# A graph network's edge sweep: edge products from TensorE taken by VectorE directly, or laid down in SBUF 40 steps ahead

## The chip, the cores and the metric

One of the eight cores of a Trainium2 chip. The metric is the device time of one execution in microseconds; lower is better. The times before are 3401.76, 3403.89 and 3417.29 us (median 3403.89). One further execution was taken by the hardware profiler.

## What is computed

6250 nodes with 256 features, 100,000 edges sorted by destination, 64 features an edge. Three rounds of messages, cut from the reference:

```python
# round 0
e = relu((x[dst] - x[src]) @ theta_w.T + theta_b + x[src] @ phi_w.T + phi_b)
out = segment_max(e, dst);  out = where(isfinite(out), out, 0)
x = layernorm(x + out)
# rounds 1 and 2
hv = x @ W_in + b_in
for W, b in ((W_u0, b_u0), (W_u1, b_u1)):
    m = relu(concatenate([hv[src], edge_attr], -1) @ W + b)
    hv = where(deg > 0, segment_max(m, dst) + hv, hv)
x = layernorm(x + relu(hv @ W_ro + b_ro))
```

Products with x[src] or hv[src] are the same for all edges of one source, so the kernel makes them once a node, as a table in DRAM with a row a node, and each edge gathers its row. Terms that depend on dst alone, and the ReLU, come after the maximum.

## The kernel before

It is written in Bass with the Tile layer, which adds the semaphore waits; under `manual_schedule` each engine runs its instructions in the order in which the program lists them. There is a prologue (the first table, a test that the edges are sorted, a branch) and then `in_order`, which this document is about; the other branch, `any_order`, doesn't run on these inputs.

**Edges.** The sorted edges are laid out in 17 blocks of 128 lanes by 56 steps (the last blocks shorter), 782 steps in all (`FS`). A lane holds consecutive edges, so a running maximum along the steps, reset by `lim` where the destination changes, leaves each segment's maximum at the segment's last edge. `sweep(r)` goes over the 782 steps once a round:

- POOL (GpSimd) issues one indirect DMA a step (`sources`, L719), which gathers 128 rows of 256 floats from `table[r]` into one slot of a `run` tile of 8 steps (`K` = 8). Gathers are listed 16 steps ahead (`AHEAD`). There are four `run` tiles, and one is used again when its write to S has landed.
- In rounds 1 and 2 the edge features' product is added. `features` (L725) loads the features of 8 steps on ACT's DMA queue, up to four tiles; `pair` (L730) makes the product of two steps with one fp32 matmul of 512 columns, into one of two PSUM buffers (tag `he`), one pair ahead; VectorE (DVE) adds it onto two steps of `run` (L923).
- DVE takes the running maximum, one instruction a step (L926).
- SyncE (SP) writes each finished group of 8 steps, 1 MB, to S in DRAM (L932).
- At a block's end `over_lanes` carries the maxima across lanes: transposes on TensorE (PE), a scan on DVE (L746), transposes back, a copy to `cs` on ACT (L758).

**Nodes.** They are treated in 49 tiles of 128. `node(t, g, b)` puts its parts into slots of the steps: `rows` (L771) gathers, on POOL, each node's row of S, at the step where its last block is written; `picks` and `carried` (L783, L790) make the carried maxima `v` with matmuls into PSUM, 3 and 2 steps before slot b; from slot b on, DVE takes the maximum of the two and ACT the ReLU, the result is added, transposed, multiplied by the next weights, and written to the next round's table on ACT's DMA queue. Round 0 also normalises, keeps the new x in `x_sb`, and makes both `hv` and the first update's table; round 2 adds `x_sb` (L853), normalises and writes the output. Tiles follow each other by `gap` = 4, 4 and 6 steps, by 3 after the last step. Whatever is left after the 782 steps is listed in slot order. A round's table must be whole before the next round's first gather.

In round 0 one more thing runs: `count`, every third step for 98 times, builds two one-hot tiles on DVE (`ol` L647, `oh` L650) and sums them on PE (L653); from the counts come `has` and `end_i`, and nodes can begin only then, at step 300.

**Memory.** x (49 tiles, 48 KB a partition) and hv (`h_sb`, the same) stay in SBUF for the whole run.

Of the kernel before, what the change touches and what calls it, by code (L numbers as in the profile page):

```python
# [17 lines left out]
P = 128  # L18
# [5 lines left out]
K = 8  # L24
# [18 lines left out]
KEPT = 7  # L43
# [11 lines left out]
SPAN = [span(t) for t in range(NT)]  # L55

# [377 lines left out]
def gnn_kernel(  # L434
# [6 lines left out]
    table = [dram.tile([ROWS, D], F32, name=f"table{r}") for r in range(3)]  # L441


    jmp = const.tile([P, P], I32)
# [7 lines left out]
    col_i = const.tile([P, P], I32)  # L452
# [97 lines left out]
def in_order(ctx: ExitStack, tc: tile.TileContext, g):  # L550
# [9 lines left out]
    heT, xTn, xn, out = (g[n] for n in ("heT", "xTn", "xn", "out"))  # L560
    ctx.enter_context(tc.manual_schedule())
# [4 lines left out]
    x_sb = one.tile([P, NT, D], F32, name="x_sb")  # L566
# [9 lines left out]
    def weight(w, name):  # L576
        t = one.tile([P, 2, D], F32, name=name)
        nc.scalar.dma_start(t, w.rearrange("(k p) f -> p k f", p=P))
        return t
# [7 lines left out]
    tb, pb = line(g["th_b"], "tb"), line(g["ph_b"], "pb")  # L587
    wcat = one.tile([P, 2, 2 * D], F32, name="wcat")
    nc.scalar.dma_start(wcat[:, :, :D], g["w_in"].rearrange("(k p) f -> p k f", p=P))
    winT = weight(g["w_inT"], "winT")  # L590
    wu0 = weight(g["w_u0"][:D, :], "wu0")
# [7 lines left out]
    whe = []  # L599
    for r, w in enumerate((g["w_u0"], g["w_u1"])):  # L600
        t = one.tile([P, 2, D], F32, name=f"whe{r}")
        nc.vector.memset(t, 0.0)
        for s in range(2):
            nc.scalar.dma_start(t[s * DE:(s + 1) * DE, s, :], w[D:, :])
        whe.append(t)
# [37 lines left out]
    def count(c):  # L643
        k = min(K, FS - c * K)
        cut = slice(c * K, c * K + k)
        ol = work.tile([P, K, P], BF16, name="ol", bufs=1)
        nc.vector.tensor_tensor(ol[:, :k, :], col.unsqueeze(1).to_broadcast([P, k, P]),  # L647
                                lo[:, cut].unsqueeze(2).to_broadcast([P, k, P]), OP.is_equal)
        oh = work.tile([P, K, NT], BF16, name="oh", bufs=1)
        nc.vector.tensor_tensor(oh[:, :k, :], col[:, :NT].unsqueeze(1).to_broadcast([P, k, NT]),  # L650
                                hi[:, cut].unsqueeze(2).to_broadcast([P, k, NT]), OP.is_equal)
        for j in range(k):
            nc.tensor.matmul(hist[:, :NT], ol[:, j, :], oh[:, j, :], start=(c == 0 and j == 0),  # L653
                             stop=(c == NG - 1 and j == k - 1))
# [50 lines left out]
    def sweep(r):  # L705
# [10 lines left out]
        def sources(s):  # L716
            if s % K == 0:
                runs[s // K] = work.tile([P, K, D], F32, name="run", bufs=4)
            nc.gpsimd.indirect_dma_start(  # L719
                out=runs[s // K][:, s % K, :], out_offset=None, in_=table[r],  # L720
                in_offset=bass.IndirectOffsetOnAxis(ap=s_s[:, s:s + 1], axis=0))

        def features(c):
            hT[c] = work.tile([P, K // 2, P], F32, name="hT", bufs=4)
            nc.scalar.dma_start(hT[c].rearrange("p q e -> p (q e)"), heT[c])  # L725

        def pair(i):
            c, q = divmod(i, K // 2)
            hp[i] = psum.tile([P, 512], F32, tag="he", name="hp")
            nc.tensor.matmul(hp[i], hT[c][:, q, :], whe[r - 1].rearrange("p s f -> p (s f)"), start=True, stop=True)  # L730
            if q == K // 2 - 1:
                del hT[c]

        def over_lanes(b, last):

            lp = psum.tile([P, 512], F32, tag="tp", name="lp")
            nc.tensor.transpose(lp[:, 2 * P:3 * P], link[:, b:b + 1].to_broadcast([P, P]), ident)
            lim2 = work.tile([P, P], F32, name="lim2")
            nc.scalar.copy(lim2, lp[:, 2 * P:3 * P])  # L739
            for k in range(2):  # L740
                nc.tensor.transpose(lp[:, k * P:(k + 1) * P], last[:, k * P:(k + 1) * P], ident)  # L741
            to, of = cT[b % 2], cT[(b + 1) % 2]

            def scan():
                for k in range(2):
                    nc.vector.tensor_tensor_scan(to[:, k, 1:], lim2, lp[:, k * P:(k + 1) * P],  # L746
                                                 of[:, k, P:] if b else 0.0, OP.min, OP.max)
                if b:
                    nc.scalar.copy(to[:, :, 0:1], of[:, :, P:])
                else:  # L750
                    nc.vector.memset(to[:, :, 0:1], 0.0)

            def back():
                cp = psum.tile([P, 512], F32, tag="tp", name="cp")
                for k in range(2):
                    nc.tensor.transpose(cp[:, k * P:(k + 1) * P], to[:, k, :P], ident)
                carried_in.append(b)
                nc.scalar.copy(cs[:, b % KEPT, :D], cp[:, :D])  # L758

            at(FIRST[b] + BLOCKS[b], scan)  # L760
            at(FIRST[b] + BLOCKS[b] + 1, back)

        def node(t, g, b):
# [22 lines left out]
            def carried():  # L786
                assert max(carried_in) - SPAN[t][0] < KEPT
                o["v"] = psum.tile([P, 512], F32, tag="v", name="v")
                for blk, p in o["pick"]:
                    nc.tensor.matmul(o["v"][:, :N1], p, cs[:, blk % KEPT, :N1], start=(blk == SPAN[t][0]),  # L790
                                     stop=(blk == SPAN[t][1]))

            def x_in():
                o["xT"] = work.tile([P, 2, P], F32, name="xT", bufs=3)
                nc.sync.dma_start(o["xT"], xTn[:, :, t * P:(t + 1) * P])
# [12 lines left out]
            def first_b():  # L808
                nc.vector.tensor_add(o["m"], o["m"], h_sb[:, t, :])
                nc.scalar.activation(o["m"], o["m"], AF.Relu, scale=has[:, t:t + 1])  # L810

            def first_c():
                nc.vector.tensor_add(o["m"], o["m"], x_sb[:, t, :])
# [4 lines left out]
            def first_e():  # L818
                norm(x_sb[:, t, :], o["m"], *o["mv"])
                o["aT"] = turned(x_sb[:, t, :])  # L820

            def first_f():
                o["g"] = times(o["aT"], wcat[:, :, D:], b2, D)

            def first_g():
                o["ps"] = times(o["aT"], wcat[:, :, :D], None, D)

            def first_h():
                new = work.tile([P, D], F32, name="new", bufs=3)
                nc.scalar.copy(new, o["g"][:, :D])  # L830
                nc.scalar.dma_start(table[1][t * P:(t + 1) * P, :], new)

            def first_i():
                nc.scalar.copy(h_sb[:, t, :], o["ps"][:, :D])

            def next_a():
                nc.vector.tensor_max(o["m"], o["m"], o["v"][:, :D])  # L837
                nc.scalar.activation(o["m"], o["m"], AF.Relu, scale=has[:, t:t + 1])
# [8 lines left out]
            def next_d():  # L847
                new = work.tile([P, D], F32, name="new", bufs=3)
# [3 lines left out]
            def last_d():  # L852
                nc.vector.scalar_tensor_tensor(o["m"], o["ps"][:, :D], 0.0, x_sb[:, t, :], OP.max, OP.add)  # L853

            def last_e():
                o["mv"] = stats(o["m"], "m")

            def last_f():
                o["y"] = work.tile([P, D], F32, name="new", bufs=3)
                norm(o["y"], o["m"], *o["mv"])  # L860
# [4 lines left out]
            at(g, rows)  # L865
            if r == 0:
# [3 lines left out]
            at(b - 3, picks)  # L870
            at(b - 2, carried)
            if r == 0:
                for i, f in ((0, first_a), (1, first_b), (3, first_c), (4, first_d), (6, first_e), (7, first_f),
                             (8, first_g), (9, first_h), (10, first_i)):
                    at(b + i, f)
            else:
                for i, f in ((0, next_a), (2, next_b), (3, next_c)):
                    at(b + i, f)
                for i, f in ((5, next_d),) if r == 1 else ((5, last_d), (6, last_e), (8, last_f), (9, last_g)):
# [3 lines left out]
        if r == 0:  # L883
# [4 lines left out]
            for i in range(NT // PART):  # L888
                at(14 + 8 * i, lambda i=i: nc.sync.dma_start(x_sb[:, i * PART:(i + 1) * PART, :],
                                                             xn[:, i * PART:(i + 1) * PART, :]))  # L890
# [5 lines left out]
        gap = (4, 4, 6)[r]  # L896
        b = 0
        for t in range(NT):
            e = max(FIRST[SPAN[t][1]] + BLOCKS[SPAN[t][1]], begin)
            b = max(b + (gap if b < FS else 3), e + 4, min(e + AHEAD + 4, FS + 4))  # L900
            node(t, max(e, b - AHEAD - 4), b)

        runs, hT, hp = {}, {}, {}
        prev = None
        blk = 0
        for s in range(-AHEAD, FS):
# [5 lines left out]
            if r > 0:  # L912
                if s == 0:
                    for i in range(4):
                        features(i)
                    pair(0)
                elif j == 0 and c + 3 < NG:
                    features(c + 3)
                if s % 2 == 0:
                    if s + 2 < FS:  # L920
                        pair(s // 2 + 1)
                    two = runs[c][:, j:j + 2, :].rearrange("p s f -> p (s f)")
                    nc.vector.tensor_add(two, two, hp.pop(s // 2))  # L923
# [18 lines left out]
    for r in range(3):  # L942
        sweep(r)
# [48 lines left out]
```

## Time and profile before

| | us |
|---|---|
| median of the runs shown | 3403.9 |
| profiled execution, own time | 4092.0 |
| its span | 4090.2 |
| PE busy (matmul) | 2032.6 (50%) |
| PE weight loads | 915.2 (22%) |
| DVE busy | 2083.0 (51%) |
| ACT busy | 280.7 (7%) |
| POOL busy | 2459.6 (60%) |
| mean granted TensorE clock | 0.667 |
| DMA | 735.87 MB, mean 180 GB/s |

The profile is one execution, and it took 688 us more than the median of the runs that weren't profiled: what it shows has to be weighed against that. Busy times are sums over all of the span. A matmul's end is modelled, not seen; an fp32 matmul appears as two records. "Issue" names idle time that ended without a release that the profile shows; "remote" names a release whose source it doesn't know. [...]

### The profile page before, as it was taken

Reading aid. Unit: us, or ns where it says so; the run is one execution under the profiler, and the core shown is the slowest. Engines: PE = TensorE matmul, PEld = TensorE weight load, DVE = VectorE, ACT = ScalarE, POOL = GpSimd, SP = SyncE. Lnnn points to the kernel's source line nnn. Section 1 sums busy time; section 2 is a strip of 40 time slices with the busy share of each in tenths; the row PEclk is TensorE's granted clock in tenths of the full one; section 3 lists DMA queues with packets and bytes.
Section 4 is the critical chain, followed back from the end, with each engine's and each line's share of the span. In section 5 each row is a group of like instructions: output and inputs, shape, how many; then the busy total and the mean of one; then the engine's idle time right before and its main releaser. Section 6 shows DMA issues by size and latency. Waiting matters only on the chain.

```text
span 4090.2 us, 22048 instructions
## 1 busy us (share of the span) xinstructions
PE 2032.6 (50%) x4957; PEld 915.2 (22%) x4957; DVE 2083.0 (51%) x4526; ACT 280.7 (7%) x770; POOL 2459.6 (60%) x2499
## 2 busy tenths in 40 slices
PE   5433444232334745455464555664455545555557
PEld 4222222111112311111121222221121212122223
DVE  2766733433334555454554454545555555555555
ACT  1000010000101100000000000110000000000001
POOL 3777755666664466566666655546666666655542
PEclk7555565555555867676777777786766777777766
DMA  6755544454554456565555555545655555555542
GB/s 223 250 195 181 195 157 169 166 181 161 170 168 147 147 189 211 172 205 179 195 192 184 181 181 183 172 164 191 204 191 193 191 180 192 182 174 171 175 146 86
DMA packets 237763, 735.87 MB, mean 180 GB/s; under 512 B 51880, under 2 KB 91799, under 8 KB 200375
## 3 DMA queue, kind: packets, MB, share of 16 engines
q0 software_dynamic: 119664, 326.92, 26.7%
q1 hardware_dynamic: 66096, 334.71, 21.5%
q10 hardware_dynamic: 51862, 72.75, 5.4%
q8 instruction: 42, 0.69, 0.1%
q14 instruction: 99, 0.80, 0.1%
HBM read 401.01 MB, written 333.16 MB: 179 GB/s over the span
## 4 chain that ended last, share of the span: by engine, by line
another core or an unknown queue 31%; DVE 18%; PE 16%; issue 15%; POOL 9%; DMA 8%; ACT 1%; ACTq 0%; DVEq 0%; POOLq 0%; SPq 0%
POOL run L719 9%; DVE run L926 8%; DVE run L923 7%; DMA run<-table,s_s 5%; PE hp L730 5%; PE prod L700 4%; PE prod L702 2%; PE v L790 2%; DMA S<-run 1%; PE ps L533 1%; PE tp L692 1%; ACT aT L694 1%; DVE pick L783 1%; DMA hT<-in_heT 0%
## 5 line engine op out<-in xcount | busy, mean ns | idle before, releaser
L719 POOL DMA_INDIRECT run<-table,s_s x2346 | 2316.6, 987 | 1294.2 <-issue 696.2
L730 PE MATMUL hp<-whe,hT 128*128 128x512 f32 x1564 | 1054.5, 779 | 589.7 <-DVE run L923 378.2
L926 DVE SCALAR_TENSOR_TENSOR run<-run,lim 128x256 f32<-128x256 f32 x2295 | 1110.6, 484 | 205.7 <-DMA run<-table,s_s 120.5
L923 DVE TENSOR_TENSOR run<-run,hp 128x512 f32<-128x512 f32 x782 | 533.7, 682 | 809.0 <-remote 459.7
L730 PEld LDWEIGHTS hp<-whe,hT 128*128 128x128 f32 x1564 | 308.0, 233 | 1190.7 <-DVE run L923 699.6
L771 POOL DMA_INDIRECT m<-S,end_i x147 | 142.4, 969 | 291.6 <-DMA S<-run 191.4
L700 PE MATMUL prod<-wcat,aT 128*128 128x256 f32 x392 | 160.4, 550 | 261.9 <-ACT aT L694 167.6
L790 PE MATMUL v<-cs,pick 128*128 128x256 f32 (+1 forms) x468 | 192.6, 540 | 123.9 <-DVE pick L783 70.9
L692 PE MATMUL tp<-ident,h_sb 128*128 128x128 f32 x196 | 52.7, 361 | 358.9 <-DVE h_sb L841 223.6
L653 PE MATMUL hist<-oh,ol 128*128 128x49 bf16 x782 | 48.8, 217 | 249.2 <-DVE oh L650 182.2
L700 PEld LDWEIGHTS prod<-wcat,aT 128*128 128x128 f32 x392 | 95.5, 268 | 314.2 <-ACT aT L694 177.6
L790 PEld LDWEIGHTS v<-cs,pick 128*128 128x128 f32 x468 | 116.2, 272 | 199.6 <-issue 83.5
L746 DVE TENSOR_TENSOR_SCAN cT<-lim,cT,lp 128x128 f32<-128x128 f32 x96 | 40.8, 468 | 218.5 <-PE lp L741 144.5
L853 DVE SCALAR_TENSOR_TENSOR m<-prod,x_sb 128x256 f32<-128x256 f32 x49 | 20.8, 424 | 248.9 <-remote 169.9
L700 PE MATMUL prod<-wro,aT 128*128 128x256 f32 x196 | 90.4, 609 | 96.8 <-issue 76.1
L647 DVE TENSOR_TENSOR ol<-col,lo 128x1024 bf16<-128x1024 bf16 x98 | 119.3, 1217 | 26.3 <-remote 25.7
L692 PEld LDWEIGHTS tp<-ident,h_sb 128*128 128x128 f32 x196 | 25.1, 173 | 451.4 <-issue 318.5
L741 PE MATMUL lp<-ident,run 128*128 128x128 f32 x102 | 28.7, 375 | 183.0 <-ACT lim L739 101.5
L700 PE MATMUL prod<-wu,aT 128*128 128x256 f32 x196 | 75.6, 524 | 68.4 <-ACT aT L694 36.7
L837 DVE TENSOR_TENSOR m<-m,v 128x256 f32<-128x256 f32 x98 | 40.5, 414 | 134.9 <-remote 78.1
L653 PEld LDWEIGHTS <-ol 128*128 128x128 bf16 x782 | 42.8, 117 | 276.2 <-DVE ol L647 164.5
L700 PE MATMUL prod<-th,xT 128*128 128x256 f32 x196 | 95.5, 640 | 8.8 <-issue 8.8
(116 smaller groups left out, 1326.0 us busy)
## 6 DMA issues: line engine op xcount, KB each, us to landing
S<-run SPq DMA_DIRECT2D x291, 1024.0 KB
hT<-in_heT ACTq DMA_DIRECT2D x196, 256.0 KB
run<-table,s_s POOLq DMA_INDIRECT x2346
table<-new ACTq DMA_DIRECT2D x98, 128.0 KB
xg<-in_xTn SPq DMA_DIRECT2D x7, 896.0 KB
table<-g SPq DMA_DIRECT2D x7, 896.0 KB
xT<-in_xTn SPq DMA_DIRECT2D x49, 128.0 KB
x_sb<-in_xn SPq DMA_DIRECT2D x7, 896.0 KB
```

The costliest lines, as they stand in the source:

```text
L533: nc.tensor.matmul(ps[:, q * D:(q + 1) * D], xg[:, k, (i + q) * P:(i + q + 1) * P], wd[:, k, :], start=(k == 0), stop=(k == 1))
L647: nc.vector.tensor_tensor(ol[:, :k, :], col.unsqueeze(1).to_broadcast([P, k, P]), lo[:, cut].unsqueeze(2).to_broadcast([P, k, P]), OP.is_e ...
L653: nc.tensor.matmul(hist[:, :NT], ol[:, j, :], oh[:, j, :], start=(c == 0 and j == 0), stop=(c == NG - 1 and j == k - 1))
L692: nc.tensor.transpose(tp[:, k * P:(k + 1) * P], a[:, k * P:(k + 1) * P], ident)
L700: nc.tensor.matmul(ps[:, :n], aT[:, k, :], w[:, k, :], start=(k == 0), stop=(k == 1 and b is None))
L702: nc.tensor.matmul(ps[:, :n], every[0:1, :], b, start=False, stop=True)
L719: nc.gpsimd.indirect_dma_start(out=runs[s // K][:, s % K, :], out_offset=None, in_=table[r], in_offset=bass.IndirectOffsetOnAxis(ap=s_s[:, ...
L730: nc.tensor.matmul(hp[i], hT[c][:, q, :], whe[r - 1].rearrange("p s f -> p (s f)"), start=True, stop=True)
L771: i = nc.gpsimd.indirect_dma_start(out=o["m"], out_offset=None, in_=S_r[:P * (FIRST[SPAN[t][1]] + BLOCKS[SPAN[t][1]]), :], in_offset=bass. ...
L790: nc.tensor.matmul(o["v"][:, :N1], p, cs[:, blk % KEPT, :N1], start=(blk == SPAN[t][0]), stop=(blk == SPAN[t][1]))
L923: nc.vector.tensor_add(two, two, hp.pop(s // 2))
L926: nc.vector.scalar_tensor_tensor(cur, prev, lim[:, s:s + 1], cur, OP.min, OP.max)
```

## The change

**Edge products.** `features` and `pair` become `products(c)`, called five groups (`EARLY` = 5, 40 steps) ahead: it loads the features of group c on SP's queue (three tiles), makes the four pairs of products on PE one after the other, and copies each from PSUM with ACT to a tile `made`, of which there are six. DVE adds four steps of `made` onto `run` with one instruction of 1024 elements, instead of two steps from PSUM with one of 512.

**Nodes.** `carried` copies `v` from PSUM to an SBUF tile (six of them) on ACT. `picks` and `carried` stand 8 and 7 steps before slot b (`calm` = 6), and the scan over lanes and its way back 5 and 6 steps after the block's end instead of 0 and 1. The ReLU with `has` moves from ACT to DVE. `hv` and the table's rows of round 0 come from one product of 512 columns. In round 2 the last ReLU is made by ACT, and the sum with x by DVE six steps later. `gap` is 6 in all rounds.

**Memory.** `x_sb` is gone: x is loaded tile by tile on SP's queue (three tiles), and round 0's result is written to a DRAM tensor `x1` on ACT's queue, and read again in round 2. Weights that are used only at the start lie in a `run` tile; the edge weights `whe` are one tile, loaded before each of the last two rounds.

The diff, cut to its core:

```diff
-KEPT = 7
+RING = 4
+EARLY = 5
+KEPT = 9
...
+def calm(s):
+    return 6
...
-        def features(c):
-            hT[c] = work.tile([P, K // 2, P], F32, name="hT", bufs=4)
-            nc.scalar.dma_start(hT[c].rearrange("p q e -> p (q e)"), heT[c])
-
-        def pair(i):
-            c, q = divmod(i, K // 2)
-            hp[i] = psum.tile([P, 512], F32, tag="he", name="hp")
-            nc.tensor.matmul(hp[i], hT[c][:, q, :], whe[r - 1].rearrange("p s f -> p (s f)"), start=True, stop=True)
-            if q == K // 2 - 1:
-                del hT[c]
+        def products(c):
+
+            hT = work.tile([P, K // 2, P], F32, tag="pt", name="hT", bufs=3)
+            nc.sync.dma_start(hT.rearrange("p q e -> p (q e)"), heT[c])
+            made[c] = work.tile([P, K, D], F32, tag="made", name="made", bufs=EARLY + 1)
+            for q in range(min(K, FS - c * K) // 2):
+                hp = psum.tile([P, 512], F32, tag="he", name="hp")
+                nc.tensor.matmul(hp, hT[:, q, :], whe.rearrange("p s f -> p (s f)"), start=True, stop=True)
+                nc.scalar.copy(made[c][:, 2 * q:2 * q + 2, :].rearrange("p s f -> p (s f)"), hp)
...
-            at(FIRST[b] + BLOCKS[b], scan)
-            at(FIRST[b] + BLOCKS[b] + 1, back)
+            e = FIRST[b] + BLOCKS[b]
+            at(e + calm(e) - 1, scan)
+            at(e + calm(e), back)
...
+                o["v"] = work.tile([P, D + 2], F32, name="vs", bufs=6)
+                nc.scalar.copy(o["v"][:, :N1], v[:, :N1])
+
+            def x_row():
+                o["x"] = work.tile([P, D], F32, name="x", bufs=3)
+                nc.sync.dma_start(o["x"], xn[:, t, :] if r == 0 else x1[t * P:(t + 1) * P, :])
...
-                nc.scalar.activation(o["m"], o["m"], AF.Relu, scale=has[:, t:t + 1])
+                nc.vector.tensor_scalar(o["m"], o["m"], 0.0, has[:, t:t + 1], OP.max, OP.mult)
...
-                norm(x_sb[:, t, :], o["m"], *o["mv"])
-                o["aT"] = turned(x_sb[:, t, :])
+                norm(o["x"], o["m"], *o["mv"])
+                o["aT"] = turned(o["x"])
+                nc.scalar.dma_start(x1[t * P:(t + 1) * P, :], o["x"])
...
             def last_d():
-                nc.vector.scalar_tensor_tensor(o["m"], o["ps"][:, :D], 0.0, x_sb[:, t, :], OP.max, OP.add)
+                o["y"] = work.tile([P, D], F32, name="new", bufs=6)
+                nc.scalar.activation(o["y"], o["ps"][:, :D], AF.Relu)
+
+            def last_dd():
+                nc.vector.tensor_add(o["y"], o["y"], o["x"])
...
-            at(b - 3, picks)
-            at(b - 2, carried)
+            at(b - late - 2, picks)
+            at(b - late - 1, carried)
...
-        gap = (4, 4, 6)[r]
+        gap = 6
...
-                if s % 2 == 0:
-                    if s + 2 < FS:
-                        pair(s // 2 + 1)
-                    two = runs[c][:, j:j + 2, :].rearrange("p s f -> p (s f)")
-                    nc.vector.tensor_add(two, two, hp.pop(s // 2))
+                if j == 0 and c + EARLY < NG:
+                    products(c + EARLY)
+                w = min(4, FS - s)
+                if s % 4 == 0:
+                    four = runs[c][:, j:j + w, :].rearrange("p s f -> p (s f)")
+                    nc.vector.tensor_add(four, four, made[c][:, j:j + w, :].rearrange("p s f -> p (s f)"))
```

## The prediction

> **What bounds the kernel now.** I read, in this order: the profile page (groups and busy times), busy time by stretch for POOL alone, the waits, and the order of time in four short windows. On the page (line, engine, operation; count; busy us, mean ns; idle us before it and what ended it) four groups carry the sweeps:
>
> ```profile
> L719 POOL DMA_INDIRECT run<-table,s_s x2346 | 2316.6, 987 | 1294.2 <-issue 696.2
> L730 PE MATMUL hp<-whe,hT 128*128 128x512 f32 x1564 | 1054.5, 779 | 589.7 <-DVE run L923 378.2
> L926 DVE SCALAR_TENSOR_TENSOR run<-run,lim 128x256 f32<-128x256 f32 x2295 | 1110.6, 484 | 205.7 <-DMA run<-table,s_s 120.5
> L923 DVE TENSOR_TENSOR run<-run,hp 128x512 f32<-128x512 f32 x782 | 533.7, 682 | 809.0 <-remote 459.7
> ```
>
> Each of the 2,346 gathers costs POOL 0.987 us and a fixed gap of 0.30 us that nothing ends ("issue": 2168 of them): 1.29 us a step. DVE needs 0.48 us a step for the running maximum and, in the last two sweeps, 0.34 us for half an edge add: 0.83 us. POOL is the slower of the two by a third. The next view gives POOL's busy time (instructions in brackets), clock, DMA share and GB/s, cut at each sweep's first and last gather:
>
> ```profile
> 0.00:59.85 59.85, 0.61 (x6) 0.98 0.70 253
> 59.85:1338.00 1278.15, 844.02 (x825) 0.53 0.53 179
> 1338.00:1389.96 51.96, 5.67 (x7) 0.90 0.24 82
> 1389.96:2663.54 1273.58, 800.95 (x825) 0.72 0.57 188
> 2663.54:2710.43 46.89, 5.67 (x6) 0.92 0.27 95
> 2710.43:4006.40 1295.97, 796.11 (x824) 0.71 0.55 184
> 4006.40:4090.20 83.80, 6.61 (x7) 0.64 0.18 64
> ```
>
> So the span is a sum on POOL: 59.9 before the first gather; 2441.1 busy in the sweeps; 2474 gaps of 0.305 = 754.6; 182.7 at the three ends; and what is left, 183 + 221 + 249 = 653 us, is POOL waiting inside the sweeps. 4090.2 in all; the profiled execution's own time is 4092.0. The median of the runs shown is 3403.9, 688 less. Without the 653 us the sum is 3437. The runs shown therefore have no room for those waits: what they hold is POOL issuing nearly without a break (3195.7), the start, and some 147 us of ends.
>
> What are the 653 us?
>
> ```profile
> DVE run L923 <- remote: 459.7, 104, 20.7
> POOL run L719 <- DVE run L926: 197.9, 47, 14.9
> POOL m L771 <- DMA S<-run: 191.4, 24, 23.3
> ...
> 1467.13 1.22 PE L730 MATMUL hp<-whe,hT 128*128 128x512 f32 x1 [3.52 <-DVE run L923]
> ...
> 1476.89 0.69 DVE L923 TENSOR_TENSOR run<-run,hp 128x512 f32<-128x512 f32 x1 [3.86 <-remote]
> ```
>
> The pair begun at 1467.13 is read, two PSUM buffers on, by the add at 1476.89: nearly 10 us for two matmul records of about 1 us. No node work stands between. These late releases push DVE behind until POOL finds no free buffer. They fill the profile, but by the sum above not the timed runs. I take them as peculiar to the profiled execution; nothing here proves it.
>
> [...] A gather takes 0.94 us when left alone, more when a two-SBUF-input operation starts just before it:
>
> ```profile
> 1397.34 1.01 DVE L926 SCALAR_TENSOR_TENSOR run<-run,lim 128x256 f32<-128x256 f32 x2
> 1397.46 1.19 POOL L719 DMA_INDIRECT run<-table,s_s  x1 [0.30 <-issue]
> ...
> 269.82 1.23 DVE L647 TENSOR_TENSOR ol<-col,lo 128x1024 bf16<-128x1024 bf16 x1 [2.68 <-remote]
> 269.97 1.90 POOL L719 DMA_INDIRECT run<-table,s_s  x1 [0.30 <-issue]
> ```
>
> The 1.23 us operation cost the gather 0.95 us: it waited for almost all that was left. [...] the equally long bf16 row above has 1.22 us (median 1.218). [...]
>
> **The change part by part.**
>
> *Edge add.* Removed: 782 adds of 128x512 with one input in PSUM (533.7 us). Added: 2 x 196 adds of 128x1024 with both inputs in SBUF, 1.22 us each, 480 us. DVE gains 54 us, worth nothing: it has 0.46 us of slack a step. [...] By the trace's stretches, POOL in 68.5 to 501.5 us, where an `ol` and an `oh` (1.22 + 0.56 us) run every third step, took 329.6 us for 292 gathers, 1.129 each; in 560 to 1338, without them, 463.2 for 481, 0.963. The difference, 0.166 x 292 = 48 us over 98 such pairs, is 0.49 us a pair; scaled to the add's share of the length, 0.34. [...] I take 0.36: 392 x 0.36 = 141 us, straight on POOL's path. Bounds 0.05 [...] to 0.55 [...]: 20 to 216 us.
>
> *Products ahead.* The same 782 matmul pairs of records, in groups of four, five groups ahead. At half clock a pair is about 1.77 us (four records in 3.54 us at 1395.74), so a group takes 7.1 us of PE per 10.3 us of POOL: hidden. Added on ACT: 782 copies 128x512 from PSUM at 0.586 us (the row `g<-ps`) = 458 us, 2.3 us per 10.3; ACT was 7% busy. What is queued behind a copy that waits for its ring slot is the node's ACT work; the slot was freed a group earlier. The 196 feature loads move from ACT's queue to SP's, where S writes queue behind them. A load waits for matmuls three groups (some 31 us) back; nothing unless PE falls that far behind.
>
> *Nodes.* 147 copies of v on ACT (0.373): hidden. 147 ReLUs (0.507) leave ACT for DVE as 147 tensor_scalar (0.417, +61 us DVE, hidden). The max with v, now from SBUF, is 147 more two-SBUF-input operations of 0.42 to 0.48 us. With the tensor_scalars and the 49 final adds that makes some 340 short holds; a short hold such as a running maximum's costs POOL about 0.02 to 0.03 us on average (0.963 against 0.946 bare): 8 us. The later slots cost nothing in the middle; seven instead of six nodes of the first two sweeps fall behind the last step, two of the seven with picks and v already done.
>
> *x in DRAM.* 7 loads of 896 KB become 98 of 128 KB on SP; 49 writes of 128 KB go on ACT's queue: 12.8 MB on top of 735.9, DMA share 0.55. At the first sweep's end a ring of three x rows chains node to node (write, then load), [...]. Ends: 0, bounds -15 to +25.
>
> Sum: +141 + 8 + 0 = +149. Against the profiled execution this stands beside the 653 us of waits, of which I expect most in the last two sweeps to go: 4092 + 149 - 400 is about 3840 for its next profile. Against the median, which does not contain them: 3403.9 + 149 = 3553.
>
> **Rivals.**
>
> *Faster.* POOL's true period is shorter than 1.25 us bare and the runs shown do contain late PE releases at L923. If the gap is 0.17 and not 0.305, 2493 x 0.136 = 340 us of the median are waits; the last two sweeps' share is 470/653, so up to 245 go, against 149 of holds: 3308. It decides from 207 us of real waits (83 ns of the period) on. For it: the waits fill the profile, and the change removes exactly their place. Against: the gap is the same 0.30 in 2168 cases, and the sum without waits meets the median within 1%.
>
> *No change.* The adds start when a gather has landed, which locks them to POOL's period; [...]: 3404. Against: the same adds' starts before lie all over the period.
>
> *A new wait.* The feature load blocks SP, S writes come late, and gathers find no buffer: 1 us a group is 196 us on top, 3749. It needs PE 31 us behind; the longest DVE wait at L923 was 20.7 us.
>
> **How the numbers follow.** The holds 0.68 (own range 3450 to 3640), faster 0.20, no change 0.08, new wait 0.04. Within 0.5% (17 us, about what a measurement of this kernel tells from no change) is the third case; so faster 0.20, same 0.08, slower 0.72. Leaving out about 1 in 10 below, in the faster case's lower half, and 1 in 10 above: 3330 to 3640.
>
> **What would show it.** Mean gather up from 0.97 to about 1.06 us in the last two sweeps and unchanged in the first; add 128x1024 at 1.22 us; POOL's waits inside the last two sweeps well under 200 us; L923's "remote" gone; profiled span down although the median rises. It is wrong if the mean gather stays at 0.97, or if the median falls with the profile.

## The result, and the profile after

The changed kernel takes 3571.1 us (median of 4 runs, 3558.3 to 3579.7), the kernel before 3410.6 beside it (3401.8 to 3419.7): a ratio of 1.047, with a 95% interval of 1.042 to 1.052. The forecast was 3553.

One thing must be known to read the numbers below. Each set of experiments ran on one chip, at one time (a "session"), and the sessions differed. In two of them, the one of this result and one later, the kernel before took 3411 and 3414 us at the median; in three others 4111 to 4126. The first kind is called quick here, the second slow. The profile of before that the prediction reads, with its 4092 us, is of the slow kind; the times beside it are of the quick one. Ratios compare runs of one session only, and leave out runs more than 1.5% above the quickest of their kernel.

The page of the changed kernel, for the groups that answer to those shown of before (line, engine, operation; count; busy us, mean ns; idle us before it and what ended it):

```profile
L730 POOL DMA_INDIRECT run<-table,s_s x2346 | 2447.2, 1043 | 833.3 <-issue 610.0
L946 DVE SCALAR_TENSOR_TENSOR run<-run,lim 128x256 f32<-128x256 f32 x2295 | 1110.6, 484 | 478.4 <-DMA run<-table,s_s 419.1
L943 DVE TENSOR_TENSOR run<-run,made 128x1024 f32<-128x1024 f32 x392 | 478.9, 1222 | 700.8 <-DMA run<-table,s_s 628.9
L742 ACT COPY made<-hp 128x512 f32<-128x512 f32 x782 | 457.6, 585 | 1382.7 <-PE hp L741 1331.5
```

The mean gather is 1.043 us where it was 0.987; this is the time of its issue on POOL, its rows land 3.2 us after the issue (median). The running maximum costs the same, the new add is 1.222 us long, and the copies by ACT are 458 us as priced. What ends most of DVE's idle time before an add is now the landing of a gather (628.9 of 700.8 us), where it was "remote" (459.7 of 809.0). Next POOL's busy time, instructions, clock, DMA share and GB/s, cut at each sweep's first and last gather:

```profile
0.00:60.39 60.39, 0.66 (x7) 0.98 0.69 250
60.39:1161.27 1100.88, 849.85 (x825) 0.56 0.63 212
1161.27:1207.68 46.41, 6.80 (x8) 0.90 0.41 130
1207.68:2317.41 1109.73, 858.67 (x825) 0.76 0.65 216
2317.41:2358.43 41.02, 7.34 (x7) 0.87 0.35 117
2358.43:3501.24 1142.81, 861.78 (x824) 0.75 0.65 214
3501.24:3556.50 55.26, 7.22 (x7) 0.69 0.29 95
```

824 gaps of 0.305 us make 251 us. In the first sweep 1100.9 - 849.9 - 251.3 leaves nothing, in the second 1109.7 - 858.7 - 251.3 leaves nothing: POOL issues without a break. In the third, 30 us are left: five of the m gathers wait for a row of S. So the span is gather issue plus the ends, and the gathers are longer. The order of time shows how (start, length, engine, operation; idle before it):

```profile
1705.43 1.23 DVE L943 TENSOR_TENSOR run<-run,made 128x1024 f32<-128x1024 f32 x1 [5.84 <-DMA run<-table,s_s]
1705.93 1.55 POOL L730 DMA_INDIRECT run<-table,s_s  x1 [0.30 <-issue]
...
1709.50 1.23 DVE L943 TENSOR_TENSOR run<-run,made 128x1024 f32<-128x1024 f32 x1 [0.67 <-DMA run<-table,s_s]
1710.29 1.26 POOL L730 DMA_INDIRECT run<-table,s_s  x1 [0.30 <-DMA run<-table,s_s]
```

A gather that starts 0.50 us into an add takes 0.60 us more than the bare 0.946, one that starts 0.79 us into it 0.31 more: both go on about 1.1 us after the add's start, just before its end.

### The profile page after: what moved, and what is told of

Its sections match the earlier page's. It is cut to its first block, busy times and chain, and to the rows that moved or that the text cites. A ratio compares the mean times of both kernels' runs of the same rounds, so it can differ in the third digit from the quotient of the medians.

```text
span 3556.5 us, 22363 instructions
## 1 busy us (share of the span) xinstructions
PE 1960.1 (55%) x4761; PEld 903.3 (25%) x4761; DVE 2100.8 (59%) x4282; ACT 723.2 (20%) x1601; POOL 2592.3 (73%) x2499
## 4 chain that ended last, share of the span: by engine, by line
POOL 19%; DMA 19%; DVE 11%; issue 10%; PE 7%; ACT 1%; ACTq 0%; DVEq 0%; SPq 0%; POOLq 0%
POOL run L730 18%; DMA run<-table,s_s 15%; DVE run L946 5%; PE hp L741 4%; DVE run L943 4%; DMA hT<-in_heT 3%; POOL m L782 1%; PE prod L711 1%; PE v L801 1%; PE prod L713 1%; PE prod L843 0%; DMA S<-run 0%; DVE m L855 0%; DVE m L856 0%; ACT aT L705 0%
## 5 line engine op out<-in xcount | busy, mean ns | idle before, releaser
L730 POOL DMA_INDIRECT run<-table,s_s x2346 | 2447.2, 1043 | 833.3 <-issue 610.0
L943 DVE TENSOR_TENSOR run<-run,made 128x1024 f32<-128x1024 f32 x392 | 478.9, 1222 | 700.8 <-DMA run<-table,s_s 628.9
L742 ACT COPY made<-hp 128x512 f32<-128x512 f32 x782 | 457.6, 585 | 1382.7 <-PE hp L741 1331.5
L741 PEld LDWEIGHTS hp<-whe,hT 128*128 128x128 f32 x1564 | 389.9, 270 | 1327.2 <-issue 663.2
L801 PE MATMUL v<-cs,pick 128*128 128x256 f32 (+1 forms) x468 | 167.0, 478 | 118.4 <-DVE pick L794 118.4
L843 PE MATMUL prod<-wcat,aT 128*128 128x512 f32 x196 | 154.0, 932 | 12.2 <-ACT aT L705 12.2
L703 PE MATMUL tp<-ident,x 128*128 128x128 f32 x98 | 29.8, 402 | 153.6 <-DVE x L698 153.0
L804 ACT COPY vs<-v 128x256 f32<-128x256 f32 (+1 forms) x147 | 54.9, 374 | 228.6 <-PE v L801 222.5
L705 ACT COPY aT<-tp 128x256 f32<-128x256 f32 x147 | 55.1, 375 | 185.7 <-PE tp L703 182.4
L711 PE MATMUL prod<-wro,aT 128*128 128x256 f32 x196 | 65.6, 465 | 25.3 <-ACT aT L705 25.3
```

The source lines that it names most:

```text
L703: nc.tensor.transpose(tp[:, k * P:(k + 1) * P], a[:, k * P:(k + 1) * P], ident)
L711: nc.tensor.matmul(ps[:, :n], aT[:, k, :], w[:, k, :], start=(k == 0), stop=(k == 1 and b is None))
L730: nc.gpsimd.indirect_dma_start(out=runs[s // K][:, s % K, :], out_offset=None, in_=table[r], in_offset=bass.IndirectOffsetOnAxis(ap=s_s[:, ...
L741: nc.tensor.matmul(hp, hT[:, q, :], whe.rearrange("p s f -> p (s f)"), start=True, stop=True)
L742: nc.scalar.copy(made[c][:, 2 * q:2 * q + 2, :].rearrange("p s f -> p (s f)"), hp)
L801: nc.tensor.matmul(v[:, :N1], p, cs[:, blk % KEPT, :N1], start=(blk == SPAN[t][0]), stop=(blk == SPAN[t][1]))
```

## The experiments

The theory: gather issue on POOL bounds the time, and an add with two inputs in SBUF makes the gather that starts during it take longer (called a hold here, as in the 0.60 and 0.31 us above); that is the 160 us. The rivals: the rest of the change (node results held over 6 steps, x and x1 in DRAM) costs the time; DVE's own length does; nothing in the gathers matters, and the late results of TensorE set the time.

| run | session | median us, all runs | before in that session | ratio, 95% interval | mean gather us |
|---|---|---|---|---|---|
| e1_add_from_psum | 1, slow | 4093.4 | 4126.1 | 0.989 (0.981 to 0.997) | 0.992 |
| e3_hold_added | 1, slow | 4191.5 | 4126.1 | 1.017 (1.009 to 1.024) | 1.046 |
| e4_no_hold | 1, slow | 4270.9 | 4126.1 | 1.037 (1.030 to 1.044) | 0.987 |
| e5_adds_of_512 | 1, slow | 4186.6 | 4126.1 | 1.014 (1.007 to 1.020) | 1.039 |
| r2_after | 2, slow | 4103.5 | 4116.9 | 0.996 (0.992 to 1.000) | 1.045 |
| r2_add_from_psum | 2, slow | 4060.2 | 4116.9 | 0.991 (0.988 to 0.994) | 0.999 |
| r2_hold_added | 2, slow | 4169.0 | 4116.9 | 1.015 (0.997 to 1.033) | 1.057 |
| r2_no_hold | 2, slow | 4273.1 | 4116.9 | 1.045 (1.032 to 1.059) | 0.984 |
| b16_before | 3, quick | 3422.0 | 3414.1 | 1.003 (1.001 to 1.005) | 0.993 |
| b16_after | 3, quick | 3557.8 | 3414.1 | 1.043 (1.040 to 1.046) | 1.051 |
| b16_add_from_psum | 4, slow | 4052.1 | 4111.2 | 0.985 (0.980 to 0.990) | 0.994 |
| psum_operands | 4, slow | 4222.7 | 4111.2 | 1.026 (1.021 to 1.031) | 0.952 |

**The edge add back on PSUM.** Products are made by pairs again, one pair ahead, and ACT's copies go with the `made` tiles; the nodes, x in DRAM and the feature loads on SP's queue stay as changed. The diff is cut to the add:

```diff
-                four = runs[c][:, j:j + w, :].rearrange("p s f -> p (s f)")
-                nc.vector.tensor_add(four, four, made[c][:, j:j + w, :].rearrange("p s f -> p (s f)"))
+                if s + 2 < FS:
+                    pair(s // 2 + 1)
+                two = runs[c][:, j:j + 2, :].rearrange("p s f -> p (s f)")
+                nc.vector.tensor_add(two, two, hp.pop(s // 2))
```

> The changed kernel with only the edge add put back: products are taken from PSUM by pairs, one pair ahead, and nothing is copied to SBUF; nodes, x in DRAM and feature loads on SP's queue stay as changed. Theory [...]: the cost goes with the add, 3571 falls by 130 to 170 us to about 3420 (3390 to 3445), and a gather in the last two sweeps takes 0.96 to 0.98 us. Rival (the nodes' new order, x in DRAM or the loads on SP's queue cost it): it stays at 3550 or more. Rival (products that aren't made 40 steps ahead let DVE wait for PE again): above 3445, with gathers at 0.97 us and waits inside the sweeps.

Measured: 4093.4 beside 4126.1. The mean gather is back at 0.992 us. The time says nothing on the 160 us, because in that session something else stands in the way:

```profile
L946 DVE TENSOR_TENSOR run<-run,hp 128x512 f32<-128x512 f32 x782 | 533.5, 682 | 1184.4 <-remote 641.1
```

DVE idled 641 us ahead of its edge adds for a release that the profile can't name. The order of time shows one case:

```profile
1699.02 1.06 PE L741 MATMUL hp<-whe,hT 128*128 128x512 f32 x1
...
1713.37 0.37 ACT L868 COPY new<-prod 128x256 f32<-128x256 f32 x1 [20.68 <-remote]
...
1718.97 0.69 DVE L946 TENSOR_TENSOR run<-run,hp 128x512 f32<-128x512 f32 x1 [19.91 <-remote]
```

ACT's copy waits for TensorE alone. The trace's semaphore events have TensorE's count rise at 1702.84, 1707.74, 1713.34 and 1718.94 us: one step every 4.9 or 5.6 us, with not one matmul record between. TensorE's results come late, by up to 20 us. The profile before has waits of the same kind.

**The hold alone, and the same DVE time without it.** Both added to the kernel before, in the last two sweeps; neither result is read.

```diff
+                if s % 4 == 0:
+                    w4 = wcat.rearrange("p k f -> p (k f)")
+                    spare = work.tile([P, K, P], BF16, name="ol", bufs=1)
+                    nc.vector.tensor_tensor(spare.rearrange("p k e -> p (k e)"), w4, w4, OP.add)
```

> The kernel before with one more DVE instruction every four steps in the last two sweeps: an add of 128x1024 with both inputs in SBUF, on a tile that nobody waits for (its result is used nowhere). Theory [...]: 392 x 0.36 to 0.43 us, so 3411 rises by 140 to 170 us to about 3565 (3520 to 3600), gathers of the last two sweeps at 1.03 to 1.08 us. Rival (the change costs through ACT's copies, queues or nodes, [...]): 3411, within 20 us, since DVE has 0.46 us of slack a step and gives 0.31 of it.

```diff
+                if s % 4 == 0:
+                    nc.vector.tensor_reduce(spare, wcat.rearrange("p k f -> p (k f)"), AX.X, OP.max)
```

> The control for the run with the added add: the kernel before with a DVE instruction of the same length every four steps, a reduction of 128x1024 to 128x1 with one SBUF input, whose result is used nowhere. Theory [...]: no change, 3411 within 20 us, gathers at 0.97 us. Rival (any 1.2 us of DVE work every four steps costs, because DVE is nearer to the bound than its busy share says): the same rise as with the added add, 140 us or more.

The gather groups of the two kernels, in this order:

```profile
L719 POOL DMA_INDIRECT run<-table,s_s x2346 | 2454.3, 1046 | 1207.9 <-issue 659.7
```

```profile
L720 POOL DMA_INDIRECT run<-table,s_s x2346 | 2315.8, 987 | 1385.2 <-issue 692.4
```

Before it was 2316.6 us. So 392 adds with two inputs in SBUF lengthen the gathers by 137.7 us, 0.35 each; 392 instructions of the same length with one such input lengthen them by nothing (-0.8). The two differ in one more thing: the reduction writes one number a partition, the add 1024. The old edge add tells these apart. It writes 512 numbers to SBUF with one input in PSUM, and gathers that start during it take the bare 0.945 to 0.946 us (b16_before, below). So it is the second SBUF input that lengthens a gather. It doesn't carry over to these times: the add costs 65 us and the reduction 145. POOL's waits inside the last two sweeps, worked out as length less busy less gaps, are 221 + 249 us in the profile before, 199 + 213 with the add, 318 + 328 with the reduction. I read this so, without a run that shows it: a longer gather is partly time that POOL would have waited anyway; more time on DVE, where TensorE's lateness has already put DVE behind, is not hidden. My expectation of "no change" for the reduction is wrong here. Why the reduction costs 80 us more than the add is open.

**The add in two halves**, in the changed kernel.

```diff
-                w = min(4, FS - s)
-                if s % 4 == 0:
+                w = 2
+                if s % 2 == 0:
```

> The changed kernel with each edge add split into two of 128x512, still with both inputs in SBUF. Theory: a gather waits for what is left of the add, so the cost goes with the square of its length: 784 adds with a hold of about 0.56 us in a period of 1.29 cost 0.12 us each, 95 us, where 392 of 1.22 cost about 150: 3571 falls by 45 to 65 us to about 3515 (3490 to 3540). Rival (the total length of such adds decides, 784 x 0.69 = 541 us against 479): 3571 to 3590.

The gathers' extra time hardly fell. It is 122 us above the profile before, and 131 in the changed kernel:

```profile
L730 POOL DMA_INDIRECT run<-table,s_s x2346 | 2438.6, 1039 | 1255.5 <-issue 668.3
L943 DVE TENSOR_TENSOR run<-run,made 128x512 f32<-128x512 f32 x782 | 535.9, 685 | 308.2 <-DMA run<-table,s_s 207.3
```

In the last two sweeps the starts of gathers are not spread evenly over these adds: of 516 gathers that start within 1 us after one, 208 start 0.15 to 0.25 us after it, where the hold costs them 1.333 - 0.946 = 0.39 us. Twice as many holds of about half the length, many of them caught early, cost nearly the same. I had expected a fall of 45 to 65 us.

**The same again, and the changed kernel itself, on another chip.**

> The changed kernel once more, beside the kernel before in the same session. In the first four experiments the kernel before took 4126 us where it had taken 3411 beside the changed kernel, so a session can be of two kinds: quick (before near 3411) or slow (before near 4126, TensorE's results arriving up to 20 us late). Theory (lateness belongs to the session, [...]): quick session 3571 us and a ratio of 1.047; slow session about 4190 us, ratio 1.015, because e5_adds_of_512, [...] took 4187, with a mean gather near 1.04 us as in the quick one. Rival (the changed kernel's ring and its 6-step slack cover the lateness): near 3571 us in either session, so a ratio of 0.87 in a slow one.

> As e1_add_from_psum: the changed kernel with its edge add put back to two adds of 128x512 that read the products from PSUM; no ring, no copies by ACT. Quick session: theory [...] 3420 us, within 0.5% of before, with a mean gather of 0.97 to 0.99 us; rival (the loss comes from the rest of the change: node results held over 6 steps, x and x1 in DRAM) 3560 us. Slow session: 4093 again, ratio 0.99.

> As e3_hold_added: the kernel before with one more add of 128x1024, both inputs in SBUF, every 4 steps in the second and third sweeps (result never read). In the slow session its gathers rose from a mean of 0.987 to 1.046 us, 138 us in all, yet the time rose by only 65. Quick session: theory (gather issue on POOL bounds the time and the hold lengthens it) 3411 + 261 x 0.36 = about 3505 to 3565 us; rival (the hold's time is swallowed by slack, or the gathers aren't the bound) within 0.5% of 3411. Slow session: 4191 again.

> As e4_no_hold: the kernel before with a reduction of 128x1024 to 128x1 (one SBUF input, 1.21 us on DVE) at the places where r2_hold_added has its add. Quick session: theory no change, 3411 within 0.5%, with a mean gather as in the kernel before; rival (DVE's own time counts, and with it the longer edge add) 3411 plus up to 392 x 1.21 = 474 us, at least above 3500. Slow session: 4271 again, where the lateness makes DVE part of the bound.

The session was slow too. The changed kernel is not immune: 4103.5 us, less than the 4190 that I expected, with its gathers as long as in the quick one (the profiled execution took 4147.5):

```profile
L730 POOL DMA_INDIRECT run<-table,s_s x2346 | 2451.4, 1045 | 1237.3 <-issue 665.4 <-DVE run L946 112.9 <-DVE run L943 93.0
```

Here it is no slower than the kernel before (0.992 to 1.000). The version with the add on PSUM, which has the rest of the change, is faster than both here, 4060.2; over the runs that the ratios use it is 31 us under the changed kernel (19 to 42). So in this slow session the ring is worth less than its hold costs, and the rest of the change gains about 1%. The two additions repeat: gathers 162 us longer than in the profile before with the add and 8 us shorter with the reduction, times 4169 and 4273.

**TensorE's load lightened.** If the late results came with TensorE's work, less work would do away with them. In bfloat16 an edge product is one matmul record of 0.593 us (mean, b16_add_from_psum), in fp32 two of 0.773 (e1_add_from_psum). The edge products in bfloat16, in both kernels (of the second only the names differ):

```diff
+                    wheb = one.tile([P, 2 * D], BF16, name="wheb%d" % r, tag="wheb")
+                    nc.vector.tensor_copy(wheb, whe[r - 1].rearrange("p s f -> p (s f)"))
...
-            nc.tensor.matmul(hp[i], hT[c][:, q, :], whe[r - 1].rearrange("p s f -> p (s f)"), start=True, stop=True)
+            nc.tensor.matmul(hp[i], hT[c].bitcast(BF16)[:, q, 1::2], wheb, start=True, stop=True)
```

> The kernel before with its edge products in bfloat16: the same hT tile read as the high halves of its numbers, against a bfloat16 copy of whe made once a sweep. So this run computes the edge products at lower precision; all else is as it was. In the slow sessions TensorE's semaphore updates come in stretches 4.9, 5.6 or 6.3 us apart with nothing recorded between them. Theory (these stretches come with TensorE's load): one instruction[...] in place of two leaves most of them out in the second and third sweeps, waits of POOL inside them fall from 221 and 249 us to under 80 each, and a slow session's 4117 us falls to 3650 to 3800 (the first sweep, which has no edge products, keeps its 180 us). Rival (the stretches don't depend on these matmuls): 4050 to 4117 us. In a quick session both say 3400, within 0.5%.

> The changed kernel with its edge products in bfloat16 in the same way (lower precision of these products, nothing else). Theory: [...]this kernel is 100 to 160 us slower than b16_before in the same session: 133 us of longer gathers and up to 30 us of waits of m's gathers for rows of S, less about 40 us at the sweeps' ends. Rival (the lateness stays, and the ring's slack pays for the hold): within 1% of b16_before, near 4100 us. In a quick session both say 3550 to 3575.

The session was quick, so it doesn't test the load; but it gives what was missing, a pair of profiles, with the change and without, in neither of which POOL waits for late results. POOL by stretch, first of b16_before, then of b16_after:

```profile
58.91:1157.10 1098.19, 846.85 (x825) 0.56 0.62 209
1157.10:1200.27 43.17, 5.95 (x7) 0.95 0.22 74
1200.27:2257.18 1056.91, 805.58 (x826) 0.53 0.68 228
2257.18:2294.60 37.42, 5.71 (x6) 0.86 0.28 90
2294.60:3346.76 1052.16, 801.15 (x824) 0.51 0.68 228
3346.76:3399.78 53.02, 6.69 (x7) 0.73 0.23 79
```

```profile
60.22:1160.86 1100.64, 849.64 (x824) 0.57 0.63 212
1160.86:1210.77 49.91, 6.85 (x7) 0.81 0.38 121
1210.77:2323.66 1112.89, 861.85 (x825) 0.52 0.65 215
2323.66:2368.81 45.15, 7.40 (x7) 0.76 0.32 106
2368.81:3497.72 1128.91, 877.84 (x825) 0.52 0.66 217
3497.72:3550.98 53.26, 7.45 (x7) 0.69 0.31 99
```

Neither kernel waits inside a sweep: 1052.2 - 801.2 - 251 is nothing, 1128.9 - 877.8 - 251 is nothing. The second sweep is longer by 56.0 us, the third by 76.8, and POOL's busy time by 56.3 and 76.7: the whole of it is gathers. The first sweep, which has no edge add, is longer by 2.4; the three ends by 6.7, 7.7 and 0.2; the start by 1.3. Sum 151.2, the difference of the spans (3551.0 - 3399.8).

**The two experiments together, and the opposite edit.** Last, the add on PSUM with the bfloat16 products, and the kernel before with fewer two-SBUF-input instructions than it has:

```diff
-                    nc.vector.tensor_add(two, two, hp.pop(s // 2))
+                    sums = hp.pop(s // 2)
+                    nc.vector.tensor_add(two if s == FIRST[blk] else sums, two, sums)
...
-                nc.vector.scalar_tensor_tensor(cur, prev, lim[:, s:s + 1], cur, OP.min, OP.max)
+                new = cur if r == 0 or s - s % 2 == FIRST[blk] else sums[:, s % 2 * D:(s % 2 + 1) * D]
+                nc.vector.scalar_tensor_tensor(cur, prev, lim[:, s:s + 1], new, OP.min, OP.max)
```

(and `ol` and `oh` compare against a copy of the column numbers in PSUM).

> The changed kernel with its edge add put back to two adds of 128x512 that read the products from PSUM (no ring, no copies by ACT), and the edge products in bfloat16 as in b16_before and b16_after (lower precision of these products, nothing else). Theory [...]: quick session 3430 us, no more than 1% over the kernel before and 125 under b16_after's 3558, mean gather 0.99 to 1.00 us; what stays over b16_before's 3422 is the 15 us at the sweeps' ends. Rival (the rest of the change costs the time): 3540 to 3560 us. Slow session: if its stretches come with TensorE's load, 3650 to 3800 us; if not, 4060.

> The kernel before, with fewer DVE instructions that have two inputs in SBUF: in the second and third sweeps the edge add writes its sums back into the PSUM tile of the products and the running maximum takes its second input from there, and in the first sweep the two comparisons that build the histogram's operands take the column numbers from a PSUM tile. Theory (only two SBUF inputs lengthen the gathers): of b16_before's 114 us above 0.946 us a gather, the 53 of the histogram's comparisons and most of the 47 in the second and third sweeps go: 3410 - 90 = 3320 us in a quick session, bounds 3310 and 3360, mean gather in the last two sweeps under 0.955 us. Rival (any overlap of DVE with a gather lengthens it, or TensorE waits for the products' tile, now held 1 us longer): 3400 to 3440 us. Slow session: 4100 to 4200 us, as the longer hold of the tile leaves TensorE less time, but with the gathers as short.

The session was slow. The first took 4052.1: with bfloat16 products TensorE's results are as late as without (4060 to 4093 with fp32), and intervals of 4.9, 5.6 and 6.3 us between rises of its count are there, 82 of them. The theory that the lateness comes with the load of the edge products has fallen: it asked for 3650 to 3800, its rival for 4060. The gathers are at 0.994, the level of the kernel before: with the add on PSUM nothing of the change lengthens them. The gathers of the second, psum_operands:

```profile
L722 POOL DMA_INDIRECT run<-table,s_s x2346 | 2234.0, 952 | 1489.0 <-issue 706.4
```

0.952 us, 83 us less in all than before, and 0.946 to 0.947 in the last two sweeps: the theory holds in this direction too. Overlapped by DVE instructions with one operand in PSUM, these gathers are at the bare length. The time, 4222.7, rose above the 4100 to 4200 that I expected; that the products' tile is held longer, which leaves TensorE less time, is my reading and was not taken apart. Whether it is faster in a quick session, as worked out, was not measured.

## Why the prediction was right, and where it was wrong

- **The bound.** "What they hold is POOL issuing nearly without a break": right. The two quick profiles and the changed kernel's first two sweeps have no waits at all, and b16_before's span of 3399.8 is what the sum without waits (3437) was to describe; the ends are 134 us, not 183.
- **The 653 us of waits.** Here a step failed: "I take them as peculiar to the profiled execution." They are not. In three of the five sessions every timed run of the kernel before, 53 in all, took 4059 to 4151 us; in the quick ones profiled runs are as quick as the rest (3401.6 is the lowest of b16_before's 12). They come with the session, for every kernel that ran in it. The experiments' four sessions were on four chips, one each, so whether it is the chip or the hour is not shown. The forecast of the median held because the times shown came from a quick session; nothing in the prediction told the two kinds apart, and that is luck. The forecast of the next profile, "about 3840", mixed the two kinds and was wrong: 3556.5 in a quick session, and a median of 4103.5 in the slow session.
- **The edge add.** 0.36 us each, 141 in all, was my estimate, near the 0.34 scaled from the first sweep's stretches. The quick pair has 133 us over the last two sweeps, 0.34 each; the hold added by itself 0.35. In the result's own profile POOL is busy 1720.5 us in these sweeps, 114 more than in b16_before: 0.29 each. The bounds, 0.05 to 0.55, were wide, and that the size came so near is partly luck. In b16_after the gathers that start during an edge add take 151 us over the bare time, 0.39 an add, but those that start during a running maximum take 25, where b16_before has 44. The hold lasts 1.1 us; with starts spread evenly over POOL's 1.29 us a step that would be 1.1 x 0.55 / 1.29 = 0.47 an add, an estimate from these two. But the starts are not even: 214 of the 361 within 1.15 us after an add come at 0.6 to 1.0 us, where a hold costs 0.2 to 0.4. In e5_adds_of_512 they crowd early, and a rule by average phase failed there. The undoing alone was not seen in a quick session; its gathers, 0.992 to 0.999 us in three slow sessions, stand for it.
- **Which instructions lengthen a gather.** The adds with two SBUF inputs did, the reductions and adds with a single one didn't: 137.7 us for the 392 adds and -0.8 for the 392 reductions, 83 us off in psum_operands, and the 133 of the quick pair. What in the chip makes the gather wait was not shown.
- **Node operations, 8 us.** A term mis-sized: about 1. In the last two sweeps of b16_after the gathers that start during a node operation take some 3 us over the bare time in all, in b16_before 2. The 147 tensor_scalars, which the prediction counted as holds, cost next to nothing: of 37 gathers of the changed kernel that start during one, 33 take 0.942 to 0.949 us, four 0.966 to 0.995. And 0.963 against 0.946 is 0.017 us for a short hold, not 0.02 to 0.03.
- **Copies, products ahead, longer DVE work.** Hidden, as forecast: no wait in the first two sweeps.
- **Ends: 0, bounds -15 to +25.** Measured +15 in the quick pair: inside the bounds, and a term mis-sized. It lies where the next sweep's first gather waits for the table's last rows: 32.5 and 26.3 us in b16_before, 39.8 and 33.9 in b16_after. Why the nodes left over take longer was not taken apart.
- **What was left out.** Some 30 us in the third sweep of the fp32 profile, m's gathers waiting for a row of S. b16_after has next to none of it (7.5 us in all, sweeps and ends), so it varies between these two.
- **The sum.** 141 + 8 + 0 = 149 forecast; 151.2 between the quick profiles, 160 between the medians of the result. No profile of the kernel before itself is from a quick session; beside b16_before, the nearest, the result's own is 156.7 us longer: 114 are gathers of the last two sweeps, 30 the wait that was left out, the rest the ends, the start and the first sweep. A hold below the forecast and a wait that it didn't have added up to nearly its sum.
- **Rivals.** *Faster* rested on late releases inside the median: in the quick profiles POOL does not wait for any, in the slow profile before its waits are 653 of the 688 us to the median, and even in a slow session the change comes out at 0.996. *A new wait* at SP did not come, but for the 30 us. *No change* needed the adds to lock to POOL's period at its harmless end; they lean to it, but don't lock.
- **Signs.** Mean gather in the last two sweeps 1.041 and 1.046 (forecast 1.06), unchanged in the first (1.030 against 1.023), the add 1.22 us: right. The "remote" is gone and the profiled span is down, but both tell the session and not the change: b16_before, without the change, has no "remote" ahead of its adds either, and a span of 3399.8.

## What to carry to other kernels

Here GpSimd's issue of indirect DMAs set the time, and moving a DVE operand from PSUM to SBUF cost 133 us in the quick pair, 0.34 an add, although the adds themselves got 55 us shorter in all (533.7 to 478.9). In a kernel of this kind, count such instructions, and read from a trace how much longer the gathers are that start during one. Before a wait in a profile is set aside, compare the profiled execution's own time with the times beside it: where they differ by a fifth, the two are of different conditions, and a forecast needs both. Slack against late TensorE results did not win back its price here: in the slow session the version without the ring was still 31 us quicker, and in the quick sessions there was nothing to win.

## What the runs showed of the hardware

- The hold follows a line. In b16_after's last two sweeps, gathers that start 0.05 to 0.2 us after an add of 1.22 us take 1.920 us on average, 0.2 to 0.4: 1.712, 0.4 to 0.6: 1.519, 0.6 to 0.8: 1.335, 0.8 to 1.0: 1.170, 1.15 to 2: 0.946. A gather waits out the add to about 1.1 us after its start. Of nine that start within the first 0.05 us, eight slip ahead of it and one waits (mean 1.062).
- In b16_before, gathers that start during an add with one input in PSUM take 0.945 to 0.946 us at every phase (356 of them).
- Sessions differ by a fifth on the same program. In the slow sessions TensorE's count rises in steps 4.9, 5.6 or 6.3 us apart, multiples of 0.7: 139 such intervals in the profile before, 147 in psum_operands, against 7, 17 and 22 in the three quick profiles (intervals within 0.05 us of these). What it is stays open; less work for TensorE does not remove it.
- The profile before, a slow one, also lacks semaphore events. Of TensorE's 2289 steps it records 1729, of DVE's 4479 it records 2803, of ACT's 764 it records 508; the changed kernel's quick one has all of them (2255, 4238 and 1573). So an interval can span a step that wasn't recorded, and the late start of those who wait, as in e1_add_from_psum, is the firmer sign.
- The granted clock of the kernel before is 0.70 to 0.72 in the quick session that has it on record and 0.66 to 0.67 in the slow sessions, 7% lower for a time that is 21% longer. With bfloat16 products it is 0.55 (b16_before, quick) and 0.54 (b16_add_from_psum, slow). A lower mean clock alone does not account for the slow sessions.
